# RWKV scan: the repeated values come from DRAM by DMA instead of through PE, and the four products of a token mix stand side by side in PE

## The chip, the cores and the metric

The program runs on one core of a Trainium2 chip. The metric is the device time of one execution in microseconds. PE is the matrix engine, DVE the vector engine, ACT the scalar engine, POOL the GpSimd engine; SP issues most DMAs. SBUF is the on-chip memory, PSUM the memory that PE writes to[...].

## What is computed

The reference applies four blocks in sequence to an activation `x` of 16 sequences x 100 steps x 512 channels, all float32: a grouped-query cross attention (layer 0), an RWKV block (layer 1), a cross attention with a feed-forward part (layer 2), and a second RWKV block (layer 3). The change touches the two RWKV blocks. Cut to what matters, such a block is

```python
xa = ln(x); sx = previous step of xa - xa
xxx = tanh((xa + sx * maa_x) @ maa_w1).reshape(b, l, 5, 32)     # five inner vectors of 32
xm = xa + sx * (maa_stack + einsum('blfd,fde->blfe', xxx, maa_w2))
xk, xw, xv, xr, xg = five slices of xm
w = exp(-exp(time_decay + tanh(xw @ td_w1) @ td_w2))
r, k, v, g = xr @ Wr.T, xk @ Wk.T, xv @ Wv.T, silu(xg @ Wg.T)
def step(s, (r_t, k_t, v_t, w_t)):                              # per head: 32 heads of 16
    a = k_t[:, None] * v_t[None, :]
    out = einsum('hi,hij->hj', r_t, u * a + s)
    return a + w_t[:, None] * s, out
x1 = x + groupnorm(out) * g @ Wo.T
return x1 + sigmoid(xr2 @ Wfr.T) * (square(relu(xk2 @ Wfk.T)) @ Wfv.T)
```

So the state of a head is a 16 x 16 matrix, and each of its 256 entries runs a linear recurrence over the 100 steps.

## The kernel before

The 16 sequences are cut into NG = 4 groups of G = 4 sequences, and the 512 channels into NC = 4 slices of 128. One tile of a group is [128, T] with T = 4 x 100 = 400 columns. `rwkv(n, ...)` builds one RWKV layer.

**Projections** (`projections(g, base)`). For a group it makes the normalised, transposed activation, the mixing input `xm`, the five inner vectors (`inner`, tanh; four of them in tile `z0` on partitions 0 to 127, the fifth in `tz`), the five mixes (`mixed(f, c)`: one matmul with 32 contraction rows for each of 5 vectors and 4 channel slices; then `scalar_tensor_tensor` on DVE into `tm` and an addition on POOL into `xj`), and the matmul chains of k, decay, v, r and g. k, v, r, w, g go to DRAM by `store` on ACT's queue, laid out [slice, 4, 32, T] so that a tile of 128 rows is contiguous.

**Units.** A chunk C is one group and one channel slice: 16 chunks of 8 units in a layer, so 128 units. In one unit u each partition scans two rows of 400 columns:

- `spread(u)` (PE): two matmuls of 32 rows with a 0/1 matrix `sel` repeat the values v over the partitions, into a PSUM tile `vb`, shifted by one step; an ACT copy writes the initial state into the first step of each sequence.
- `product(u)` (DVE): `vb` times the repeated k (`kr`), in place in PSUM, 128 x 792.
- `scan(u)`: two `tensor_tensor_scan` on DVE, reading the repeated decay `wr` and `vb`, writing SBUF tile `a`; then one POOL multiplication of `a` by the repeated r (`rr`), 128 x 800.
- `gather(p)` (PE): four matmuls for a pair of units, summing into the PSUM bank `acc`.

`repeat(C, rp)` fetches `kr`, `wr`, `rr` from DRAM: for each of the three, four DMAs of 32 partitions. `enter(C)` fetches the unrepeated tiles `vc`, `kc`, `rc`; `gates` fetches `gc`. `bonus` and `norm` add the u term and the group norm, with POOL multiplications `rk`, `og`, `gc`.

**Order.** The loop over u starts at -42 and writes every engine's program order by hand: DVE, ACT, POOL and PE instructions go through wrappers (line 77 for DVE, ACT and POOL, line 82 for matmuls, line 85 for transposes) that keep program order. In each unit the loop emits `spread(u + 1)`, `product(u)`, the deferred readers of PSUM banks, `scan(u)`, the loads of the next chunk, `gather`, and then as many filler pieces of PE work (projections of the next group, output projection, and in the last 34 units the channel-mixing half) as a budget `due` allows: 2.5, 2.95 or 3.9 us of PE work a unit. Group 0's projections stand before unit 0; the last group's channel mixing follows unit 127. PSUM holds two `vb` tiles of two banks, `acc`, and three banks `mm` for everything else, taken in turn by `Slots`.

Of the kernel before, what the change touches and what calls it, by code (L numbers as in the profile page):

```python
# [35 lines left out]
def xattn_sequence(ctx: ExitStack, tc: tile.TileContext, d: dict, out: bass.AP):  # L36
# [42 lines left out]
    vector, scalar, gpsimd = InOrder(nc.vector), InOrder(nc.scalar), InOrder(nc.gpsimd)  # L79
# [80 lines left out]
    class Slots:  # L160
# [22 lines left out]
        def read_later(self, bank, fn):  # L183
            once = self.readers[id(bank)] = self.defer(1, fn)
            return once
# [450 lines left out]
    def rwkv(n, ws, next_weights, last):  # L636
# [6 lines left out]
        with ExitStack() as es:  # L643
# [6 lines left out]
            vbs = [psum.tile([128, 2, 512], F32, name=f"vb{i}") for i in range(2)]  # L650
            acc = psum.tile([128, 512], F32, name="acc")
            slots = Slots([psum.tile([128, 512], F32, name=f"mm{i}") for i in range(3)])
# [3 lines left out]
            w2a = one.tile([128, E], F32, name="maa_w2a")  # L656
            nc.sync.dma_start(out=w2a, in_=d[f"L{n}_maa_w2"][0:128, :])

            w2b = one.tile([96, E], F32, name="td_maa_w2")
            nc.sync.dma_start(out=w2b[:64], in_=d[f"L{n}_td_w2"])  # L660
            nc.sync.dma_start(out=w2b[64:], in_=d[f"L{n}_maa_w2"][128:160, :])
# [26 lines left out]

            fold = one.tile([128, 32], F32, name="fold")
            nc.vector.tensor_reduce(fold, ident.rearrange("p (r s) -> p s r", s=32), AX.X, ALU.add)  # L690
            sel = one.tile([128, 16, 32], F32, name="sel")
            for j in range(16):
                nc.vector.tensor_copy(
                    sel[:, j, :].rearrange("p (h i) -> p h i", i=16),
                    fold.rearrange("p (h j) -> p h j", j=16)[:, :, j : j + 1].to_broadcast([128, 2, 16]),
                )
# [101 lines left out]

            def projections(g, base):
                nm = f"{n}_{g}"  # L800
                to = put[g] = {
                    t: dram.tile([NC, 4, 32, T], F32, tag=t, name=f"d{t}_{nm}")
                    for t in ("k", "v", "r", "w", "g")
                }

                def store(t, c, tile):
                    nc.scalar.dma_start(out=to[t][c].rearrange("r p t -> (r p) t"), in_=tile)
# [48 lines left out]
                def inner(lo, hi):  # L856
                    p0, z = (0, "z0") if lo == 0 else (64, "tz")
                    rs = slice(p0, p0 + hi - lo)
                    chain(
                        2.7, late, None, soon, lambda ps: ps[rs, :T], lambda c: w1[:, c, lo:hi],  # L860
                        lambda c: st["xm"][:, c, :],
                        lambda ps: scalar.activation(st[z][rs, :], ps[rs, :T], AF.Tanh),
                    )

                def mixed(f, c):

                    if c == 0:
                        xj[f] = two.tile([128, NC, T], F32, tag="xm", bufs=3, name=f"xj_{nm}_{f}")
                    ps = slots.bank()
                    cols = slice(c * 128, (c + 1) * 128)  # L870
                    rs = slice(32 * f, 32 * f + 32) if f < 4 else slice(64, 96)
                    w, z = (w2a, st["z0"]) if f < 4 else (w2b, st["tz"])
                    mm(out=ps[:, :T], lhsT=w[rs, cols], rhs=z[rs, :], start=True, stop=True)

                    def read():
# [6 lines left out]
                    mixes[f].append(slots.read_later(ps, read))  # L882
# [61 lines left out]
                mix = lambda f, c: piece(0.67, lambda: mixed(f, c), late)  # L944
                inner(0, 128)
                mix(0, 0)
                inner(128, 160)
                for c in range(1, NC):
                    mix(0, c)
                mix(1, 0)  # L950
                mix(1, 1)
                plain(0, "Wk", "k", 0)
                plain(0, "Wk", "k", 1)
                mix(1, 2)
                plain(0, "Wk", "k", 2)
                mix(1, 3)
                plain(0, "Wk", "k", 3)
                mix(2, 0)
                decay_in()
                for c in range(NC):  # L960
                    if c:
                        mix(2, c)
                    piece(0.67, lambda c=c: decay(c), late)
                for f, w, t in ((2, "Wv", "v"), (3, "Wr", "r")):
                    for c in range(NC):
                        mix(f + 1, c)
                        plain(f, w, t, c)
# [3 lines left out]
            def channels(g, slot):  # L971
# [41 lines left out]
                def keys(co):  # L1013
                    def read(ps):
                        if co == 0:
                            st["kk"] = two.tile([128, NC, T], F32, tag="kk", bufs=1, name=f"kk_{nm}")
# [19 lines left out]
                def values(i):  # L1036
                    b = g * G + i

                    def read(ps):
                        def add():  # L1040
# [3 lines left out]
                            if last:  # L1044
                                nc.sync.dma_start(out=out[b], in_=xb[b])
# [43 lines left out]
            def enter(C):  # L1089
# [4 lines left out]
                for k, bufs in (("v", 2), ("k", 1), ("r", 1)):  # L1094
                    t[k] = two.tile([128, T], F32, tag=f"{k}c", bufs=bufs, name=f"{k}c_{n}_{C}")
                    nc.sync.dma_start(out=t[k], in_=put[g][k][c].rearrange("r p t -> (r p) t"))
                repeat(C, 0)

            def repeat(C, rp):
                g, c = C // NC, C % NC  # L1100
                rep = chunks[C]["rep"][rp] = {}
                for t in ("k", "w", "r"):
                    rep[t] = two.tile([128, 2, T], F32, tag=f"{t}rep", bufs=3, name=f"{t}r_{n}_{C}_{rp}")
                    for jq in range(4):
                        nc.sync.dma_start(
                            out=rep[t][32 * jq : 32 * jq + 32],
                            in_=put[g][t][c, 2 * rp : 2 * rp + 2].rearrange("r p t -> p r t"),
                        )
# [23 lines left out]
            def spread(u):  # L1132

                C, jg, rp = where(u)
                p4 = vbs[u % 2][:, :, :T].rearrange("p r (b t) -> p r b t", t=L)
                for i in range(2):
                    rs = slice(64 * rp + 32 * i, 64 * rp + 32 * i + 32)
                    mm(
                        out=p4[:, i, :, 1:L], lhsT=sel[rs, 4 * jg : 4 * jg + 4, :].rearrange("p q m -> p (q m)"),
                        rhs=steps(chunks[C]["v"][rs, :])[:, :, 0 : L - 1], start=True, stop=True,  # L1140
                    )
                g = C // NC
                scalar.copy(
                    p4[:, :, :, 0], s0r[:, 2 * rp : 2 * rp + 2, C % NC, jg, g * G : (g + 1) * G]
                )

            def product(u):
                C, jg, rp = where(u)
                p4 = vbs[u % 2][:, :, :T].rearrange("p r (b t) -> p r b t", t=L)
# [6 lines left out]
            def scan(u):  # L1156
                C, jg, rp = where(u)
                rep = chunks[C]["rep"][rp]
                a = products[u] = two.tile([128, 2, T], F32, tag="a", bufs=4, name=f"a_{n}_{u}")
                for i in range(2):  # L1160
                    vector.tensor_tensor_scan(
                        a[:, i, :], rep["w"][:, i, :], vbs[u % 2][:, i, :T], 0.0, ALU.mult, ALU.add
                    )
# [39 lines left out]
            def gates(C):  # L1203
# [4 lines left out]
                nc.sync.dma_start(out=chunks[C]["g"], in_=put[g]["g"][c].rearrange("r p t -> (r p) t"))  # L1208
# [22 lines left out]
            while u < UNITS + 6 or pieces or slots.due:  # L1231
# [15 lines left out]
                if u == UNITS - 32 - 3:  # L1247
                    cm.update(load(n, "Wfk", "Wfr", "Wfv"))
                if u >= UNITS and not nws and not any(p[3] == ("wo", NG - 1) for p in pieces):
                    nws.update(next_weights())  # L1250
                unit = 0 <= u < UNITS
                if 0 <= u + 1 < UNITS:
                    spread(u + 1)
# [6 lines left out]
                if 0 <= C < NC * NG:  # L1260
                    if at == 4:
                        enter(C)
                    elif at == 6:
# [433 lines left out]
```

## Time and profile before

| | |
|---|---|
| median of 3 runs | 3563.27 us (3559.06 to 3570.37) |
| the profiled execution, its time | 3563.91 us |
| its span | 3561.8 us |
| PE busy | 3252.8 us (91% of the span) |
| DVE busy | 1768.5 us (50%) |
| POOL busy | 1374.2 us (39%) |
| ACT busy | 972.8 us (27%) |
| DMA | 213.26 MB, mean 60 GB/s |
| units of layer 1 | first product at 859.5 us, last scan ends at 1506.3 us |
| units of layer 3 | first product at 2819.4 us, last scan ends at 3465.5 us |

The busy time of an engine is the union of its instructions over the span[...]. The table's shares are means over stages with different limits; a stage is read from its own window. A group of the profile is named out<-in with the tiles of the program, "vb<-vc,sel" for instance is the matmul of `spread`. A float32 matmul appears as two instructions.

### The profile page before, as it was taken

The numbers are of one execution on the slowest core, as the hardware profiler recorded it, in microseconds if no ns is written. First come the engines' busy times: TensorE is split into PE (matmuls) and PEld (weight loads), VectorE is DVE, ScalarE is ACT, GpSimd is POOL, SyncE is SP. The second block draws the span as 40 slices with busy tenths as digits, with TensorE's granted clock in tenths as the row PEclk, the third lists the DMA queues.
The fourth block names the chain that finished last, engine by engine and source line by source line (L and its number), as shares of the span: only waits on it lengthen the run. The fifth ranks groups of instructions, "written<-read, shape, count | busy, mean of one in ns | idle before, by whom it ended". The sixth has DMA issues, their size and how long they took to land. (4 is left out here: it accounts for less than half of the span.)

```text
span 3561.8 us, 45408 instructions
## 1 busy us (share of the span) xinstructions
PE 3252.8 (91%) x17411; PEld 1434.5 (40%) x17411; DVE 1768.5 (50%) x3570; ACT 972.8 (27%) x1699; POOL 1374.2 (39%) x1036
## 2 busy tenths in 40 slices
PE   6999998868999988989999999699998899998898
PEld 3444443334333333334455455344443433333333
DVE  4777777723767755523333333400001386775551
ACT  1323222322333333322222322201111233333332
POOL 1444444543666655412212112200002366665541
PEclk8999999978999989989999999899998899998998
DMA  5010101022434342011000010200011243434300
GB/s 167 21 30 21 30 21 33 1 65 82 134 101 136 116 130 77 14 52 35 19 19 19 27 31 21 74 0 0 0 47 49 83 138 101 136 116 119 86 27 16
DMA packets 151074, 213.26 MB, mean 60 GB/s; under 512 B 22942, under 2 KB 131294, under 8 KB 150858
## 3 DMA queue, kind: packets, MB, share of 16 engines
q1 hardware_dynamic: 127818, 177.59, 17.3%
q10 hardware_dynamic: 23040, 32.78, 2.6%
q8 instruction: 137, 2.24, 0.3%
q14 instruction: 79, 0.65, 0.1%
HBM read 174.25 MB, written 36.04 MB: 59 GB/s over the span
## 5 line engine op out<-in xcount | busy, mean ns | idle before, releaser
L77 POOL TENSOR_TENSOR a<-a,rr 128x800 f32<-128x800 f32 x256 | 480.5, 1878 | 342.1 <-DVE a L77 265.4
L77 DVE TENSOR_TENSOR_SCAN a<-wr,vb 128x400 f32<-128x400 f32 x512 | 475.7, 970 | 19.3 <-PE acc L82 9.7
L77 DVE TENSOR_TENSOR vb<-vb,kr 128x792 f32<-128x792 f32 x256 | 250.5, 979 | 197.1 <-ACT vb L77 195.5
L77 DVE CUSTOM_DVE_ANT_0 junk<-l_sc,mask 100x361 f32<-100x361 f32 x512 | 273.0, 533 | 89.9 <-PE l_sc L82 73.4
L82 PE MATMUL vb<-vc,sel 32*128 32x396 f32 x1024 | 260.8, 566 | 2.4 <-ACT th L77 1.3
L77 DVE TENSOR_TENSOR pt<-l_sc,maskT 121x400 f32<-121x400 f32 x384 | 193.5, 566 | 91.9 <-PE l_sc L82 91.0
L77 ACT ACTIVATE pt<-pt 121x1600 f32<-121x1600 f32 x96 | 147.6, 1538 | 284.2 <-DVE pt L77 282.6
L1425 DVE CUSTOM_DVE_ANT_0 junk<-l2a_sc,mask 100x361 f32<-100x361 f32 x256 | 136.9, 535 | 173.0 <-PE l2a_sc L82 155.8
L63 PE MATMUL p<-l_proj,h 128*100 128x512 f32 x512 | 220.4, 593 | 0.0
L77 POOL TENSOR_TENSOR xj<-tm,ext 128x400 f32<-128x400 f32 x160 | 152.5, 960 | 170.3 <-DVE tm L77 165.2
L77 DVE SCALAR_TENSOR_TENSOR tm<-mm,vec,sx 128x400 f32<-128x400 f32 x160 | 99.8, 631 | 229.3 <-PE mm L82 184.3
L1617 DVE TENSOR_TENSOR x<-p,x 100x512 f32<-100x512 f32 x16 | 11.1, 691 | 379.3 <-PE p L63 340.2
L1461 POOL TENSOR_TENSOR pa<-pt,pt 121x1600 f32<-121x1600 f32 x16 | 57.2, 3573 | 366.7 <-ACT pt L1456 366.7
L63 PE MATMUL h<-yTb,l_fc 128*128 128x400 f32 x512 | 175.4, 505 | 7.9 <-ACT yTb L229 7.9
L82 PE MATMUL v<-l_v_w,ct 128*121 128x512 f32 x384 | 179.9, 614 | 0.0
L82 PE MATMUL k<-ct,l_k_w 128*128 128x361 f32 x512 | 172.8, 481 | 7.7 <-DVE mv_l2a L207 7.7
L77 POOL TENSOR_TENSOR pa<-pt,pt 121x1600 f32<-121x1600 f32 x32 | 114.7, 3583 | 167.0 <-ACT pt L77 167.0
L82 PE MATMUL l_sc<-kz,qz 32*100 32x361 f32 x1024 | 116.0, 523 | 42.6 <-DVE pt L77 21.6
L77 ACT COPY vb<-s0r 128x8 f32<-128x8 f32 x256 | 43.1, 168 | 408.7 <-PE vb L82 318.6
L82 PEld LDWEIGHTS vb<-vc,sel 32*128 32x128 f32 x1024 | 85.3, 190 | 145.5 <-issue 105.3
L63 PEld LDWEIGHTS p<-l_proj,h 128*100 128x100 f32 x512 | 85.7, 167 | 133.2 <-issue 132.6
L63 PEld LDWEIGHTS h<-yTb,l_fc 128*128 128x128 f32 x512 | 98.4, 193 | 82.9 <-ACT yTb L229 9.8
(254 smaller groups left out, 5317.3 us busy)
## 6 DMA issues: line engine op xcount, KB each, us to landing
kr<-dk SPq DMA_DIRECT2D x256, 100.0 KB
wr<-dw SPq DMA_DIRECT2D x256, 100.0 KB
rr<-dr SPq DMA_DIRECT2D x256, 100.0 KB
ct<-in_ctxT SPq DMA_DIRECT2D x32, 722.0 KB
dk<-k ACTq DMA_DIRECT2D x32, 200.0 KB
kc<-dk SPq DMA_DIRECT2D x32, 200.0 KB
dw<-wd ACTq DMA_DIRECT2D x32, 200.0 KB
dv<-v ACTq DMA_DIRECT2D x32, 200.0 KB
```

The lines of the kernel that those rows point to most:

```text
L63: nc.tensor.matmul(out=ps, lhsT=lhs(c), rhs=rhs(c), start=(c == 0), stop=(c == n - 1))
L77: return lambda *args, **kw: tc.keep_in_program_order(op(*args, **kw))
L82: pin(nc.tensor.matmul(**kw))
L1425: nc.vector.tensor_tensor_reduce(out=junk, in0=ss[r][:L, :S2], in1=t["mask"], scale=-1.0, scalar=FLT_MAX, op0=ALU.add, op1=ALU.min, accum_ ...
L1461: nc.gpsimd.tensor_tensor(t["pa"], t["pt"][0], pt, ALU.add)
L1617: nc.vector.tensor_tensor(x, ps[:L, :], x, ALU.add)
```

## The change

- `spread` goes. `fetch(u)` on SP's queue reads v from DRAM, every row 16 times, straight into the SBUF tile `a` of the unit, two units ahead; `a` has 6 buffers instead of 4. v lies in DRAM shifted by one element and in another row order, so that its store and its plain load are four DMAs of 32 partitions each. `first(u)` writes the initial state into `a` with ACT, one unit ahead. `product` and both scans now work in place in `a`.
- k, r, w, g lie in DRAM as [slice, 32, 4, T]. `repeat` fetches each repeated tile with one DMA, the fourfold repetition being the outermost dimension of its DRAM access, and the six of a chunk are spread over five units.
- A mix is one piece: `hidden(f)` copies the 32 rows of an inner vector onto the four groups of 32 partitions by four DMAs, and `mixed(f)` issues the four slices' matmuls on the four groups into four banks, one behind the other. The weights `w2a` are laid out to match. The readers of the banks are spread over two units.
- The PSUM of `vb` becomes four more banks for the turn: 7 instead of 3.
- DMAs inside the loop go through a wrapper that keeps SP's program order. Three weight matrices of the channel mixing are loaded in quarters over twelve units. `kk` shares the buffers of `xm`; `vc` has one buffer; the matrix `sel` is no longer built. The `due` budgets are as before.

```diff
-            vbs = [psum.tile([128, 2, 512], F32, name=f"vb{i}") for i in range(2)]
-            slots = Slots([psum.tile([128, 512], F32, name=f"mm{i}") for i in range(3)])
+            slots = Slots([psum.tile([128, 512], F32, name=f"mm{i}") for i in range(7)])
...
+            def rows_of(g, t, c):
+                if t == "v":
+                    n0 = 1 + c * 128 * T
+                    rows = put[g]["v"][n0 : n0 + 128 * T].rearrange("(j h r t) -> r h j t", h=2, r=4, t=T)
+                    return [(slice(32 * r, 32 * r + 32), rows[r]) for r in range(4)]
+                return [(slice(0, 128), put[g][t][c].rearrange("p r t -> r p t"))]
...
-                    t: dram.tile([NC, 4, 32, T], F32, tag=t, name=f"d{t}_{nm}")
-                    for t in ("k", "v", "r", "w", "g")
+                    t: dram.tile([NC, 32, 4, T], F32, tag=t, name=f"d{t}_{nm}")
+                    for t in ("k", "r", "w", "g")
...
-                    nc.scalar.dma_start(out=to[t][c].rearrange("r p t -> (r p) t"), in_=tile)
+                    for ps, rows in rows_of(g, t, c):
+                        nc.scalar.dma_start(out=rows, in_=tile[ps])
...
+                def hidden(f):
+                    z = st["z0"][32 * f : 32 * f + 32, :] if f < 4 else st["tz"][64:96, :]
+                    t = st["zr", f] = two.tile([128, T], F32, tag="zr", bufs=2, name=f"zr_{nm}_{f}")
+                    for c in range(NC):
+                        sync.dma_start(out=t[32 * c : 32 * c + 32, :], in_=z)
+
+                def mixed(f):
...
+                    for c, ps in enumerate(banks):
+                        rs = slice(32 * c, 32 * c + 32)
+                        mm(out=ps[:, :T], lhsT=w2a[rs, f, :], rhs=st["zr", f][rs, :], start=True, stop=True)
...
-            def repeat(C, rp):
-                rep = chunks[C]["rep"][rp] = {}
-                for t in ("k", "w", "r"):
+            def repeat(C, rp, names):
+                rep = chunks[C]["rep"].setdefault(rp, {})
+                for t in names:
                     rep[t] = two.tile([128, 2, T], F32, tag=f"{t}rep", bufs=3, name=f"{t}r_{n}_{C}_{rp}")
-                    for jq in range(4):
-                        nc.sync.dma_start(
-                            out=rep[t][32 * jq : 32 * jq + 32],
-                            in_=put[g][t][c, 2 * rp : 2 * rp + 2].rearrange("r p t -> p r t"),
-                        )
+                    k = put[g][t][c, :, 2 * rp : 2 * rp + 2, :]
+                    sync.dma_start(
+                        out=rep[t], in_=bass.AP(k.tensor, k.offset, [[0, 4], [4 * T, 32], [1, 2 * T]])
+                    )
...
-            def spread(u):
-                p4 = vbs[u % 2][:, :, :T].rearrange("p r (b t) -> p r b t", t=L)
-                for i in range(2):
-                    rs = slice(64 * rp + 32 * i, 64 * rp + 32 * i + 32)
-                    mm(
-                        out=p4[:, i, :, 1:L], lhsT=sel[rs, 4 * jg : 4 * jg + 4, :].rearrange("p q m -> p (q m)"),
-                        rhs=steps(chunks[C]["v"][rs, :])[:, :, 0 : L - 1], start=True, stop=True,
-                    )
+            def fetch(u):
+                a = products[u] = two.tile([128, 2, T], F32, tag="a", bufs=6, name=f"a_{n}_{u}")
+                v = put[g]["v"]
+                n0 = v.offset + ((c * 16 + 4 * jg) * 8 + 2 * rp) * T
+                sync.dma_start(out=a, in_=bass.AP(v.tensor, n0, [[4 * T, 8], [0, 16], [1, 2 * T]]))
+
+            def first(u):
                 scalar.copy(
-                    p4[:, :, :, 0], s0r[:, 2 * rp : 2 * rp + 2, C % NC, jg, g * G : (g + 1) * G]
+                    products[u].rearrange("p r (b t) -> p r b t", t=L)[:, :, :, 0],
+                    s0r[:, 2 * rp : 2 * rp + 2, C % NC, jg, g * G : (g + 1) * G],
                 )
...
-                    vector.tensor_tensor_scan(
-                        a[:, i, :], rep["w"][:, i, :], vbs[u % 2][:, i, :T], 0.0, ALU.mult, ALU.add
-                    )
+                    vector.tensor_tensor_scan(a[:, i, :], rep["w"][:, i, :], a[:, i, :], 0.0, ALU.mult, ALU.add)
                 gpsimd.tensor_tensor(a, a, rep["r"], ALU.mult)
...
+                if 0 <= u + 2 < UNITS:
+                    fetch(u + 2)
                 if 0 <= u + 1 < UNITS:
-                    spread(u + 1)
+                    first(u + 1)
                 if unit:
                     product(u)
...
                     if at == 4:
                         enter(C)
+                    elif at == 5:
+                        repeat(C, 0, "w")
                     elif at == 6:
-                        repeat(C, 1)
+                        repeat(C, 0, "r")
                         bonus(C, 0)
                     elif at == 7:
+                        repeat(C, 1, "kw")
                         bonus(C, 1)
                 C = u // 8
+                if 0 <= C < NC * NG and at == 0:
+                    repeat(C, 1, "r")
```

## The prediction

> **What bounds the kernel now.** I read the page's busy times first (PE 91%), then the stretches of the units, because only the RWKV layers change. Layer 1's units 0 to 92, then 93 to 127, all instructions; columns are busy us of PE, PEld, DVE, ACT, POOL, then granted clock, DMA share, GB/s:
>
> ```profile
> 859.40:1285.90 426.50, 412.32 (x1560) 156.37 (x1561) 312.97 (x385) 136.01 (x288) 283.44 (x228) 0.94 0.41 120
> 1285.90:1506.40 220.50, 196.00 (x665) 72.51 (x664) 127.03 (x158) 77.57 (x150) 117.34 (x99) 0.90 0.21 57
> ```
>
> The first stretch is PE's: 412 of 426 us, 4.59 us a unit (426.5 / 93). The second takes 6.30 us a unit (220.5 / 35). Layer 3 repeats both within 1 us. The same stretch for `vb` on PE, for the product (with `kr`), and for four of the five mixes (`z`, PE first):
>
> ```profile
> 859.40:1285.90 426.50, 94.55 (x372) 0.94 0.41 120
> 859.40:1285.90 426.50, 91.00 (x93) 0.94 0.41 120
> 859.40:1285.90 426.50, 44.68 (x96) 15.00 (x96) 1.51 (x3) 0.94 0.41 120
> ```
>
> So the spread costs PE 1.02 us a unit. The mixes cost 44.7 us, plus a quarter for the fifth vector: 56 us, 0.60 a unit. DVE (313) and POOL (283) have room, and run side by side: together 6.4 us of work in 4.59 us. That rests on `vb` being in PSUM. Where a DVE instruction has both inputs in SBUF, the timeline shows something else:
>
> ```profile
> 1350.32 1.88 POOL L77 TENSOR_TENSOR a<-a,rr 128x800 f32<-128x800 f32 x1 [0.96 <-DVE a L77]
> 1351.67 1.08 DVE L77 SCALAR_TENSOR_TENSOR x<-th_1b,x 100x512 f32<-100x512 f32 x1
> 1352.15 1.48 POOL L77 TENSOR_TENSOR gc<-gc,og 128x400 f32<-128x400 f32 x1
> 1352.67 1.85 DVE L77 TENSOR_TENSOR_SCAN a<-wr,vb 128x400 f32<-128x400 f32 x2
> ```
>
> `x<-th_1b,x` normally takes 0.69 us. Here it ends 0.55 us after POOL's `a` (1352.20), and `gc`, normally 1.06, ends 0.88 us after it. They take turns, with about 0.15 us of overlap at a handover. The scans, whose `vb` is in PSUM, make nobody wait.
>
> Last, the DMAs. One store of 100 rows, then one weight load of 512 rows, each alone; I show packets and the load's GB/s by slice:
>
> ```profile
> DMA packets 110, 0.20 MB, mean 34 GB/s; under 512 B 10, under 2 KB 10, under 8 KB 110
> DMA packets 528, 1.05 MB, mean 150 GB/s; under 512 B 16, under 2 KB 16, under 8 KB 528
> GB/s 0 0 0 0 0 0 0 140 105 187 187 293 176 257 293 363 386 410 421 421 421 386 398 410 328 211 152 47 0 0 0 0 0 0 0 0 0 0 0 0
> ```
>
> The small packets are one completion for each DMA engine used: 10 engines for 100 rows, 16 for 512 (128 partitions). At the peak 16 engines move 421 GB/s, 26.3 GB/s each.
>
> [...]
>
> **The change, part by part.**
>
> *PE.* It loses 1.02 us a unit of spread and three quarters of the mixes (0.45): 4.43 busy - 1.47 = 2.96 us a unit. Before unit 0, 20 mix calls of 0.94 us become 5, less waits for the new copies: I take -8 us a layer (-14 to +4). Building `sel` (16 copies of 0.17 us) was off the path: nothing.
>
> *DVE and POOL.* Product and scans now read two SBUF inputs. Their own durations I keep: product 0.98 us, two scans 1.85 us. [...] But they exclude POOL's 283.4 / 93 = 3.05 us: 2.83 + 3.05, less three handovers of 0.15, is 5.4 us a unit; in the last 35 units POOL has 117.3 / 35 = 3.35, so 5.7. Bounds: no exclusion for scans at one end (then DVE's own 3.4), no overlap and some gaps at the other (6.2).
>
> *DMA: the largest term.* For each new access I take the leading dimension. A repeated tile, [4 x 32 x 800]: 4 engines. A fetch, [8 x 16 x 800]: 8. k, r, w, g in and out, [4 x 32 x 400]: 4. v in and out, [2 x 16 x 400]: 2. [...] per chunk each of them carries:
>
> - six repeated tiles of 409.6 KB / 4: 614 KB
> - eight fetches of 409.6 KB / 8: 410 KB
> - `kc`, `rc`, `gc`, 204.8 KB / 4 each: 154 KB
> - v's plain load, 204.8 KB / 2: 102 KB
> - while projections run, four stores / 4 and v's / 2: 205 + 102 KB
>
> The sum is 1587 KB, at 26.3 GB/s 60 us for 8 units, 7.5 us a unit. Without stores it is 1280 KB, 49 us, 6.1 a unit. Before, every one of these used 16 engines (32 or 128 leading rows), hence a DMA share of 0.41 only. The new mean, some 0.95 MB a unit, looks harmless as well; it is the uneven split that counts. If instead all DMAs used 16 engines, 0.95 MB at 421 GB/s is 2.3 us a unit and hidden.
>
> *Waits and queues.* Product now waits for `first` on ACT, and that for the fetch. Behind it on ACT stand the tanh, the copies of k, v, r and the store issues; PE's banks and SP's `hidden` wait for those. SP is one ordered queue: a fetch waits for the gather of the unit six before, and the second `kr`, `wr` for the scan just before their issue, so the queue cannot always be kept full. SP's issue count stays about the same (28 a chunk before, 26 with 5 of `hidden`, at 0.4 us). The `hidden` copies have 32 leading rows, 16 engines, 0.1 us each: small. The quartered weight loads carry the same bytes. `kk` in the `xm` ring and the single `vc` wait only for readers long done: nothing, and one unit's wait if that cover goes.
>
> *Sum.* I add 10% for gaps in the DMA rings (0 to 25%), a choice, since PE's queue before kept 97% and a chain of DMA, compute and buffer release should do worse: 8.25 us a unit, then 6.7. Per layer: 93 x (8.25 - 4.59) = +340; 35 x (6.7 - 6.3) = +14; before unit 0: -8. About +348, twice +696. The tail after unit 127 is unchanged. The profiled execution took 3563.9 us (span 3561.8; median of the runs 3563.3), so 3563.9 + 696 = **4260 us**. With no gaps 93 x 2.91 - 35 x 0.2 - 14 = +250 a layer, about 4060; with 25% (9.4 and 7.6) about 4550.
>
> **The rivals.** *Turns only:* the DMAs do spread, or the engines chosen rotate, and DVE and POOL set the pace. 93 x (5.4 - 4.59) - 35 x 0.6 - 8 = +46 a layer up to 93 x (6.2 - 4.59) - 8 = +142: 3656 to 3848, about **3720**. For it: the turns are in the trace[...].
>
> *Faster:* DMAs spread and scans don't exclude POOL. Then DVE's 3.4 us plus some turns of the product alone, about 3.9 us a unit, replaces PE's 4.59, and the last 35 units lose the spread (about -1.0): -64 - 35 - 8 = -107 a layer, about **3350**. It decides where both new prices are below 4.59 us a unit. Against it: the scan has two SBUF inputs like `x<-th_1b,x`.
>
> *The mixes don't stand side by side:* PE keeps 0.45 us a unit, still below 3.5, and nothing moves in the first two cases.
>
> **How the numbers follow.** Few engines 0.70, turns only 0.20, faster 0.10. The point is the first case's 4260; its own range is 4060 to 4500. The 8-in-10 range reaches down over the turns case: 3650 to 4500. About 0.3% is what a measurement of this kernel can tell from no change. Faster by more 0.09, within 0.02, slower by more 0.89.
>
> **What would show it.** Few engines: on ACT's queue each of the 128 stores of k, r, w, g counts 128 + 4 packets and each of the 128 parts of v 32 + 2, in all 128 x 132 + 128 x 34 = 21248 (160 x 144 = 23040 before; 24576 if all used 16 engines). Pace near 8 us a unit, `first` or the product waiting for the fetch, DMA share under 0.5. Turns: product and POOL's `a` above 0.98 and 1.88 us in the mean. A pace below 4.6 us refutes both; 5.4 to 6.2 with the small counts would say that the split is right and its price wrong.

## The result, and the profile after

The changed kernel takes **4384.8 us** (median of 4 runs, 4378.6 to 4399.1), the kernel before beside it 3564.2 us. The ratio is 1.231 (95% interval 1.227 to 1.234): 821 us slower. The profiled execution has a span of 4380.6 us, against 3561.8.

The time is lost in the units of the two RWKV layers. These are the stretches of layer 1's units 0 to 92 and 93 to 127 in the changed kernel, with the columns of the prediction's first fence (busy us of PE, PEld, DVE, ACT, POOL, then granted clock, DMA share, GB/s):

```profile
860.90:1660.80 799.90, 377.61 (x1222) 145.31 (x1222) 417.26 (x388) 140.33 (x298) 354.39 (x235) 0.70 0.34 116
1660.80:1912.20 251.40, 179.38 (x522) 68.08 (x522) 160.55 (x156) 77.08 (x151) 148.50 (x100) 0.78 0.35 116
```

No engine is near full: PE 378 of 800 us, DVE 417, POOL 354, and the DMA share is 0.34. (DVE and POOL together are busy for 772 us, so turns between these two could fill the stretch as well; e5 below decides that.) A unit takes 799.9 / 93 = 8.60 us instead of 4.59, and in the second stretch 251.4 / 35 = 7.18 instead of 6.30. From the first product to the last scan, layer 1 takes 1051.3 us (1912.2 - 860.9) instead of 646.8, layer 3 1067.3 instead of 646.1: 404.5 + 421.2 = 826 us, which is the whole loss.

Three groups of the page (busy us, mean ns of one, idle before them and what ended most of it):

```profile
L77 DVE TENSOR_TENSOR_SCAN a<-wr,a 128x400 f32<-128x400 f32 x512 | 684.9, 1378 | 237.3 <-ACT a L77 125.9
L77 POOL TENSOR_TENSOR a<-a,rr 128x800 f32<-128x800 f32 x256 | 534.7, 2093 | 681.4 <-DMA rr<-dr 386.7
L77 DVE TENSOR_TENSOR a<-a,kr 128x792 f32<-128x792 f32 x256 | 321.9, 1257 | 625.3 <-DMA a<-dv 425.4
```

The same three in the kernel before:

```profile
L77 DVE TENSOR_TENSOR_SCAN a<-wr,vb 128x400 f32<-128x400 f32 x512 | 475.7, 970 | 19.3 <-PE acc L82 9.7
L77 POOL TENSOR_TENSOR a<-a,rr 128x800 f32<-128x800 f32 x256 | 480.5, 1878 | 342.1 <-DVE a L77 265.4
L77 DVE TENSOR_TENSOR vb<-vb,kr 128x792 f32<-128x792 f32 x256 | 250.5, 979 | 197.1 <-ACT vb L77 195.5
```

DVE and POOL do take turns now: the three groups are busy for 209, 54 and 71 us longer. But the idle time before them grew by more, 218, 339 and 428 us. For POOL's `a` and the product most of it ends with a DMA, for the scans half of it with ACT's copy. A selection of the waits (us in total, times, longest); the lines with SPq are from the waits of SP's queue:

```profile
ACT a L77 <- DMA a<-dv: 1015.6, 144, 23.1
PE mm L82 <- POOL rk L77: 513.6, 30, 30.1
DVE a L77 <- DMA a<-dv: 425.4, 89, 17.4
POOL a L77 <- DMA rr<-dr: 386.7, 32, 20.7
...
SPq L77 <- PE acc L82: 328.2, 45, 19.1
...
SPq L77 <- DMA a<-dv: 118.7, 56, 12.0
...
SPq L77 <- DMA wr<-dw: 90.9, 22, 7.6
SPq L77 <- DMA rr<-dr: 88.0, 18, 6.9
```

The fetches `a<-dv` are late, the repeated `rr` too. `PE mm <- POOL rk` is the bonus' matmul: it was 17.8 us in all before. SP's `PE acc` is a fetch that waits for a gather to free its buffer of `a`. The last three lines, 298 us together, are SP waiting for other DMAs to land, although its next DMA does not need their data. The semaphore events in the trace tell why: the 1274 DMAs that SP and ACT issue share eight semaphores, and in all 1266 pairs that follow each other on one semaphore the first had landed before the second's issue ended. So at most eight DMAs were in flight. In units 0 to 92 of layer 1 all eight were for 27% of the time, in the kernel before for 1%. One slow DMA held up issues that had nothing to do with it.

The timeline shows how these hang together:

```profile
988.47 11.69 ACTq L813 DMA_DIRECT2D dv<-v  x4
...
997.62 1.87 POOL L77 TENSOR_TENSOR a<-a,rr 128x800 f32<-128x800 f32 x1
...
999.02 1.30 DVE L77 TENSOR_TENSOR a<-a,kr 128x792 f32<-128x792 f32 x1 [10.39 <-DMA a<-dv]
1000.20 0.20 ACT L77 COPY a<-s0r 128x8 f32<-128x8 f32 x1 [14.58 <-DMA dv<-v]
1000.30 0.62 ACT L77 ACTIVATE kc<-kc,vec 128x400 f32<-128x400 f32 x1
...
1001.00 1.24 POOL L77 TENSOR_TENSOR rk<-rc,kc 128x400 f32<-128x400 f32 x1 [1.52 <-ACT kc L77]
...
1002.30 1.70 PE L82 MATMUL mm<-rk,ones 128*128 128x400 f32 x2 [19.84 <-POOL rk L77]
...
1003.93 1.56 PE L82 MATMUL acc<-a,gat 128*32 128x400 f32 x8
...
1010.08 1.28 SPq L77 DMA_DIRECT2D a<-dv  x1
```

DVE waited 10.4 us for a fetch, ACT 14.6 us before its `first`. In that time ACT issued four stores of v, 0.6 us each, and waited for DMAs to land between them: the third started at 998.94, just after a fetch had landed at 998.92. Behind `first` on ACT stands `kc`, behind that POOL's `rk`, then PE's bonus matmul, which held PE's ordered queue for 19.8 us. The gather follows, and only later does SP issue the next fetch. A late DMA thus delays the release of the buffer for a later one. POOL's and DVE's first lines also show a turn: the product, 0.98 us alone, ends 0.83 us after POOL's `a` (999.49).

Last, the row of the page for ACT's DMA queue (packets, MB, share):

```profile
q10 hardware_dynamic: 21248, 32.77, 2.2%
```

21248 packets is the count that the prediction worked out for 4 and 2 engines. That the leading dimension sets this number, and that all such DMAs meet on the same few engines, was its author's assumption: no DMA of SP or ACT in the kernel before has fewer than 11 semaphore events. The semaphore events of the trace after bear out the first. A DMA with a leading dimension of 2, 4 or 8 has one event more than that: 3 for each part of v, 5 for each repeated tile and for each store and plain load of k, r, w, g, 9 for each fetch. A copy of `hidden`, with 32, has 16, as all DMAs of k, v, r, w, g have in the kernel before; a load or store of 100 rows has 11.

The packets' times say how busy the few engines were. (During the prediction's lone store and weight load, ten and sixteen packets at a time were the commonest counts above zero, as many as their small packets.) In units 0 to 92 of layer 1 at least one packet was under way for 98% of the time, exactly four for 44% and more than eight for 9%. While no DMA in flight led with more than 4 (81 us of the stretch), four packets or fewer were under way for 85% of the time and never more than seven, although the leading dimensions of those in flight added up to 18.6 in the mean. While the largest was 8 (470 us), eight or fewer were for 93%, never more than twelve, with a mean sum of 29.9. So these DMAs did not add up, as if they shared their engines. Which engine carried a packet the trace does not say.

### The profile page after: what moved, and what is told of

The parts are those of the page before. It is cut to its first block, busy times and chain, and to the rows that moved or that the text cites. A ratio compares the mean times of both kernels' runs of the same rounds, so it can differ in the third digit from the quotient of the medians.

```text
span 4380.6 us, 43662 instructions
## 1 busy us (share of the span) xinstructions
PE 3094.9 (71%) x16387; PEld 1381.0 (32%) x16387; DVE 2041.9 (47%) x3536; ACT 967.7 (22%) x1699; POOL 1567.8 (36%) x1036
## 3 DMA queue, kind: packets, MB, share of 16 engines
q1 hardware_dynamic: 134138, 290.61, 19.8%
q10 hardware_dynamic: 21248, 32.77, 2.2%
## 5 line engine op out<-in xcount | busy, mean ns | idle before, releaser
L77 DVE TENSOR_TENSOR_SCAN a<-wr,a 128x400 f32<-128x400 f32 x512 | 684.9, 1378 | 237.3 <-ACT a L77 125.9
L77 POOL TENSOR_TENSOR a<-a,rr 128x800 f32<-128x800 f32 x256 | 534.7, 2093 | 681.4 <-DMA rr<-dr 386.7
L77 DVE TENSOR_TENSOR a<-a,kr 128x792 f32<-128x792 f32 x256 | 321.9, 1257 | 625.3 <-DMA a<-dv 425.4
L82 PE MATMUL mm<-rk,ones 128*128 128x400 f32 x64 | 54.2, 950 | 513.6 <-POOL rk L77 513.6
L77 ACT COPY a<-s0r 128x8 f32<-128x8 f32 x256 | 51.6, 202 | 1319.7 <-DMA a<-dv 1015.6
L77 POOL TENSOR_TENSOR xj<-tm,ext 128x400 f32<-128x400 f32 x160 | 202.4, 1288 | 110.7 <-DVE tm L77 110.7
L82 PE MATMUL acc<-a,gat 128*32 128x400 f32 x1024 | 166.9, 619 | 56.0 <-POOL a L77 52.4
L82 PE MATMUL acc<-rk,center 128*32 128x400 f32 x256 | 44.7, 787 | 222.2 <-ACT sq L77 222.2
L82 PEld LDWEIGHTS mm<-rk,ones 128*128 128x128 f32 x64 | 16.1, 313 | 533.7 <-POOL rk L77 533.7
L82 PE MATMUL mm<-xj,l_Wk 128*128 128x400 f32 x256 | 108.1, 565 | 59.5 <-POOL xj L77 59.2
```

The lines of the kernel that those rows point to most:

```text
L77: return lambda *args, **kw: tc.keep_in_program_order(op(*args, **kw))
L82: pin(nc.tensor.matmul(**kw))
```

## The experiments

The pace below is in us a unit, units 0 to 92, then 93 to 126, of layer 1, worked out from the starts of the products in each trace. "DMA on 16 engines" means that the leading dimension of its access in DRAM is 16 or 32; the packet counts of e1 and e2 below show 16 completions for each such DMA.

| run | us | ratio (95%) | pace |
|---|---|---|---|
| before | 3564 | 1 | 4.59, 6.28 |
| after | 4384.8 | 1.231 (1.227–1.234) | 8.60, 7.26 |
| e1_repeats16 | 4182.1 | 1.173 (1.165–1.181) | 7.97, 6.57 |
| e8_loads_stores16 | 4333.0 | 1.216 (1.212–1.219) | 8.23, 7.44 |
| e2_all16 | 3967.1 | 1.113 (1.108–1.117) | 6.73, 6.38 |
| e5_no_r_multiply | 4355.6 | 1.222 (1.218–1.226) | 8.49, 7.39 |
| e6_all16_no_r_multiply | 3843.3 | 1.078 (1.075–1.081) | 6.18, 6.02 |
| e7_all16_gather_first | 3952.2 | 1.109 (1.106–1.112) | 6.69, 6.27 |
| e9_all16_first_on_dve | 3959.4 | 1.109 (1.107–1.112) | 6.70, 6.47 |
| e10_all16_first_dve_late_bonus | 3971.1 | 1.113 (1.111–1.116) | 6.73, 6.53 |
| e11_after_first_on_dve | 4359.9 | 1.223 (1.220–1.226) | 8.49, 7.22 |
| e12_all16_old_shapes | 3893.4 | 1.092 (1.090–1.094) | 6.44, 6.45 |
| e3_scan_from_sbuf | 3688.4 | 1.034 (1.030–1.039) | 5.13, 6.59 |
| e4_mix_pairs_on_before | 3508.7 | 0.984 (0.979–0.989) | 4.50, 6.07 |

### Are the few engines the cause? e1, e2

e1 is the changed kernel with each repeated tile loaded by four DMAs of 32 partitions:

```diff
-                    sync.dma_start(
-                        out=rep[t], in_=bass.AP(k.tensor, k.offset, [[0, 4], [4 * T, 32], [1, 2 * T]])
-                    )
+                    for jq in range(4):
+                        sync.dma_start(out=rep[t][32 * jq : 32 * jq + 32], in_=k)
```

> Only the repeated tiles (kr, wr, rr) go back to four DMAs of 32 partitions each, from the new DRAM layout, so that their leading dimension is 32 and 16 engines take them; everything else is the changed kernel. Few engines: [...] the turns of DVE and POOL (5.4 to 6.2 us) are next. Pace 5.6 to 6.6 us a unit, time about 3850 us (3700 to 4000). If the bytes or the wait for the fetch are what costs, whatever the spread: unchanged at about 4385 us, since the same bytes move.

e2 adds the same for every other short leading dimension. v is stored twice, so that the fetch leads with 16:

```diff
-                    return [(slice(32 * r, 32 * r + 32), rows[r]) for r in range(4)]
-                return [(slice(0, 128), put[g][t][c].rearrange("p r t -> r p t"))]
+                    return [
+                        (slice(32 * r + 16 * h, 32 * r + 16 * h + 16), rows[i, r, h])
+                        for i in range(copies) for r in range(4) for h in range(2)
+                    ]
+                return [(slice(32 * r, 32 * r + 32), put[g][t][c, :, r, :]) for r in range(4)]
...
-                sync.dma_start(out=a, in_=bass.AP(v.tensor, n0, [[4 * T, 8], [0, 16], [1, 2 * T]]))
+                sync.dma_start(out=a, in_=bass.AP(v.tensor, n0, [[4 * T, 16], [0, 8], [1, 2 * T]]))
```

> As the run with the repeated tiles on 16 engines, and all other DMAs too: k, r, w, g stored and loaded by four DMAs of 32 partitions; v stored twice in DRAM, so that a fetch's leading dimension is 16 (16 rows, each read 8 times), its parts stored and loaded by 16 partitions. Few engines: 7.8 MB a chunk over 16 engines is 486 KB each, 18.5 us or 2.3 us a unit, so DMA no longer sets the pace and the turns of DVE and POOL do: 5.4 to 6.2 us a unit, 3656 to 3848 us, about 3750; products and scans stay longer than 0.98 and 0.97 us in the mean. Without turns: below 4.6 us a unit, about 3350 us. If bytes or the wait for the fetch cost: 4385 us or more, since a second copy of v is stored.

Measured: 4182 and 3967 us. So 203 us come back with the repeated tiles alone, 418 with all DMAs spread: half of the loss. Both misses are on the same side: e1 was expected at 3850 and e2 in the turns' range up to 3848. ACT's queue in e2 tells that the spreading happened, 40960 packets:

```profile
q10 hardware_dynamic: 40960, 39.39, 3.6%
```

512 parts of 32 rows (k, r, w, g) with 16 completions each and 512 parts of 16 rows (v, twice) with 16 each give just that: 512 x 48 + 512 x 32.

The same row for SP's queue, after, e1, e2:

```profile
q1 hardware_dynamic: 134138, 290.61, 19.8%
```

```profile
q1 hardware_dynamic: 145658, 290.66, 24.9%
```

```profile
q1 hardware_dynamic: 157306, 290.70, 28.6%
```

The 11520 packets that e1 adds are 192 repeated tiles with 64 completions instead of 4. The 11648 that e2 adds are 256 fetches (16 instead of 8), 96 loads of k, r and g (64 instead of 4) and 32 of v (128 instead of 8). So the repeated tiles and the fetches, too, ran on the 4 and 8 engines for which the prediction had no trace.

SP's row for the fetches in the tile view of `a` (min, median and max ns of one issue) shows the pressure going away. After, e1, e2:

```profile
L77 SPq DMA_DIRECT2D a<-dv x256: 574/804/7382, 833.4 to 4272.2; - x128
```

```profile
L77 SPq DMA_DIRECT2D a<-dv x256: 574/592/705, 839.9 to 4060.6; - x128
```

```profile
L77 SPq DMA_DIRECT2D a<-dv x256: 513/519/829, 847.8 to 3854.8; - x128
```

In the changed kernel one issue took up to 7.4 us. Where ACT waited for a fetch, the time from the end of its issue to ACT's copy was 13.6 us in the median after, 6.8 in e1, 4.2 in e2.

### Which of the few-engine DMAs? e8

The changed kernel with only the stores and plain loads spread (the second `return` of e2's edit, with v in parts of 16 rows stored once, and `gc` to match).

> The changed kernel with only the stores and the plain loads of k, r, w, g and v spread over 16 engines (four DMAs of 32 partitions, v eight of 16); repeated tiles stay on 4 engines and fetches on 8. [...] as in the run with the repeated tiles on 16 (1127 KB). If the load of the busiest engines is what counts: about the same time as there, 4180 us, within 80. If it is the place in SP's queue (v's and the plain loads in front of the fetch of the chunk's last unit, a hole of some 16 us in the product's pace there): that hole shrinks below 9 us and the time goes to 4050 us or less.

4333 us: 52 of the 821. Neither number was met. By the prediction's kind of sum, e1 and e8 leave nearly the same bytes on the busiest engines while projections run: for e1, 410 (fetches) + 154 (repeated tiles / 16) + 154 + 102 (loads) + 307 (stores) = 1127 KB a chunk; for e8, 614 + 410 + 51 + 64 = 1139 KB. At 26.3 GB/s that is 5.4 us a unit for either. They took 7.97 and 8.23 us in the first stretch. (In the second, without the stores, e8 has more on these engines, 1075 KB against 820, and is slower, 7.44 against 6.57.) So the sum is wrong for both. Either the load of the busiest engines is not what counts, or 26.3 GB/s, read from one weight load, is too high a rate. SP's row for e8 beside those above speaks for the rate:

```profile
q1 hardware_dynamic: 143738, 290.65, 22.2%
```

The bytes are the same in all four, the packets' time is not: 19.8% of 16 engines over the span is 13.9 ms, and 16.6 in e1, 15.4 in e8, 18.1 in e2. A busy engine thus moved 20.9, 17.5, 18.9 and 16.0 GB/s in the mean. An estimate from these rates puts the busiest engines at 9.5 us a unit in the changed kernel, 8.1 in e1 and 7.5 in e8; measured were 8.60, 7.97 and 8.23. At least one packet was under way for 92% of the first stretch in e1 and in e8. So the load of the busiest engines fits within some 10% again, at a lower rate, and is not ruled out. Why packets take longer when more engines are at work is not shown.

The place in SP's queue may count beside the load: e8 left the median from a fetch's issue to ACT's copy at 13.5 us, e1 halved it.

### Do DVE's and POOL's turns set the pace? e3, e5, e6

e3 is the kernel before with the product writing to SBUF, so that only the scans have two SBUF inputs (their v still comes through PE and PSUM):

```diff
-                    p4[:, :, :, 1:L], p4[:, :, :, 1:L],
+                    products[u].rearrange("p r (b t) -> p r b t", t=L)[:, :, :, 1:L], p4[:, :, :, 1:L],
...
-                        a[:, i, :], rep["w"][:, i, :], vbs[u % 2][:, i, :T], 0.0, ALU.mult, ALU.add
+                        a[:, i, :], rep["w"][:, i, :], a[:, i, :], 0.0, ALU.mult, ALU.add
```

> The kernel before, with PE's spread kept: only the product writes its result into the SBUF tile a (5 buffers) instead of in place into PSUM, so that the two scans have two SBUF inputs; kk shares the buffers of xm to make room. Product still has one input in PSUM. Turns: the scans and POOL exclude each other; 1.85 + 3.05 less two handovers of 0.15 is 4.6 us a unit, just at PE's 4.59, so the mean scan grows to 1.1 us or more, POOL's a above 1.95, and the time to 3580 to 3700 us. No turns for scans: scan 0.97 us, POOL's a 1.88 us and the time 3564 us within 0.5%.

3688 us, as expected: +123. The groups of its page:

```profile
L77 DVE TENSOR_TENSOR_SCAN a<-wr,a 128x400 f32<-128x400 f32 x512 | 687.5, 1382 | 8.7 <-ACT sq L77 0.5
L77 POOL TENSOR_TENSOR a<-a,rr 128x800 f32<-128x800 f32 x256 | 483.4, 1889 | 378.7 <-DVE a L77 307.6
L77 DVE TENSOR_TENSOR a<-vb,kr 128x792 f32<-128x792 f32 x256 | 245.9, 961 | 181.7 <-PE vb L82 131.8
```

A scan grew from 970 to 1382 ns when its second input moved from PSUM to SBUF. The SBUF input alone doesn't slow it: the 150 scans that overlap no POOL instruction took 968 ns in the mean (993 at most), the other 362 took 1554; before, both kinds took 968 to 971. POOL's `a` stayed at 1889 ns, the product, with one input in PSUM, at 961. So a scan with two SBUF inputs takes turns with POOL, which for scans was the prediction's assumption.

e5 and e6 leave out the multiplication by r on POOL (one column of each row is set to zero instead), in the changed kernel and in e2:

```diff
-                gpsimd.tensor_tensor(a, a, rep["r"], ALU.mult)
+                gpsimd.memset(a[:, :, 0:1], 0.0)
```

> The changed kernel with POOL's multiplication of a by the repeated r left out (256 instructions of 1.88 us; POOL writes one column of a instead, which reads nothing; rr is still loaded). It asks whether, in the changed kernel, the DMA engines or the turns set the pace. Few engines: [...] the time stays above 4150 us. Turns: DVE's 2.83 us and POOL's other 1.2 us are 4.0 us a unit, and up to 256 x 1.9 = 480 us go: 3900 to 3950 us.

> The run with all DMAs on 16 engines, again without POOL's multiplication by r. There the turns should set the pace of 6.6 us a unit, or else SP's ordered queue does. Turns: 4.0 us a unit of DVE and POOL together, PE 3.0, so 4.2 to 5.0 us a unit and 3450 to 3650 us. Ordered queue (fetches wait for gathers that stand on PE behind the product of the bonus, and behind loads that wait): pace stays above 6 us a unit, 3850 us or more.

Without the multiplication the changed kernel gains 29 us, e2 gains 124. The turns are there in both, but in the changed kernel DVE and POOL take them in time that they would spend waiting for DMAs. That decides between the prediction's case and its first rival: with few engines, DMA sets the pace. It also says that e2's remaining 402 us are not mainly turns with POOL's `a`: 280 of them remain in e6.

### What holds e2 at 6.7 us a unit? e7, e9, e10, e11, e12

With all DMAs on 16 engines and a turns price of 5.4, something still costs 1.3 us a unit. I tried four single suspects.

e7 issues PE's gather right behind the scan, ahead of the next chunk's loads and the bonus, so that buffers come free earlier:

```diff
+                if u % 2 and 0 <= (u - 3) // 2 < UNITS // 2:
+                    gather((u - 3) // 2)
```

> The run with all DMAs on 16 engines, with the gather issued right behind the scan of its unit, ahead of the next chunk's loads and of the bonus product, which waits on PE for POOL's rk (288 us in that run) with the gather, and so the next fetch, behind it. Ordered queue: the loop fetch - ACT - rk - bonus product - gather - next fetch opens, the pace goes from 6.6 to 5.6 - 6.2 us a unit, 3750 to 3880 us. Turns alone: 3967 us within 1%.

e9 moves the copy of the step-0 column from ACT to DVE, away from ACT's store issues; e11 does that to the changed kernel. The copy stands just ahead of its unit's product:

```diff
-                if 0 <= u + 1 < UNITS:
-                    first(u + 1)
                 if unit:
+                    first(u)
                     product(u)
...
-                scalar.copy(
+                vector.tensor_copy(
```

> e2_all16 (3967.1 us) with the copy of the step-0 column moved from ACT to DVE, behind the product of its own unit, so that no scan stands behind ACT's store issues (16 parts of v: 9.3 us each time on ACT). In e2 DVE waited 238.0 us for ACT's copy in the scans; the copy adds 256 x some 0.1 us to DVE. If ACT's order is what keeps e2 above the turns' price: 3967 - 238 + 26 = 3755, at most 3850. If SP's one ordered queue does it (its repeated tiles, loads and fetches, each with waits): 3930 or more, with the waits gone over to the fetch.

> The changed kernel (4384.8 us) with that copy moved from ACT to DVE alone; the DMAs stay on few engines. There ACT waited 1015.6 us for the fetch before the copy. If the few engines set the pace, DVE waits for the same fetches instead: 4300 to 4400. If ACT's order behind its stores and copies is the cost, 4250 or less.

e10 is e9 with the bonus two units later:

```diff
-                        bonus(C, 0)
                     elif at == 7:
                         repeat(C, 1, "kw")
-                        bonus(C, 1)
...
                     repeat(C, 1, "r")
+                    bonus(C, 0)
+                if 0 <= C < NC * NG and at == 1:
+                    bonus(C, 1)
```

> The kernel of e9 with the bonus' first two steps (POOL's rk, PE's product of it) issued at units 0 and 1 of their own chunk instead of units 6 and 7 of the chunk before, which is when their loads have just been asked for. In e2 PE waited 287.7 us for rk, and SP's fetches waited 285.7 us for PE's gathers (buffers of a). If that chain (late load, rk, PE, gather, buffer, fetch) costs time: 60 to 150 us under e9. If the fetches' own place in SP's queue decides, within 20 us of e9.

e12 is e9 with the DRAM layout of the kernel before for k, r, w, g, and v stored there a third time for its plain load, so that these stores and the plain loads are one DMA each on 16 engines:

```diff
-                return [(slice(32 * r, 32 * r + 32), put[g][t][c, :, r, :]) for r in range(4)]
+                return [(slice(0, 128), put[g][t][c].rearrange("r p t -> (r p) t"))]
...
-                    for ps, rows in rows_of(g, t, c, 2):
+                    for ps, rows in rows_of(g, t, c, 2) + (rows_of(g, "vp", c) if t == "v" else []):
```

> The kernel of e9 with k, r, w and g laid out in DRAM as in the kernel before, and v stored there once more in that layout for its plain load: still 16 engines for every DMA, but one DMA of 128 rows where e9 has four or eight. SP then issues some 5.0 DMAs a unit instead of 7.04 (3.14 us of issue a unit in e9, expected 2.2), ACT 21 a chunk instead of 32. If the number of issues in SP's one queue holds the fetches back, 0.9 us a unit over 2 x 93 to 2 x 128 units: 3959 - 170 to - 230, so 3730 to 3790, a pace near the turns' 5.4. If it is the waits between them in a fixed order (for the gathers' buffers, the stores to DRAM, the scans' tiles), 3900 or more.

Measured: e7 -15 us against e2; e9 -8, or 0.2%, too little to build on; e10 +12 against e9; e11 -25 against the changed kernel. In e9, DVE's waits for ACT's copy and for the fetch fell from 238.0 + 97.9 = 336 us to 167.3, and the time did not follow: in layer 1, DVE's waits for PE at `rk` and `tm` rose from 52 to 100 us. In e11 they were 513.7 us, against 125.9 + 425.4 = 551 in the changed kernel. All three theories of a single wait fell; e11 came out as the few-engine theory had it. It also tells against the chain through `kc`: with `first` gone from ACT, PE still waited 479.5 us for `rk`, against 513.6.

e12 gained 66 us on e9, where fewer issues were to bring 170 to 230, and lies just under the 3900 of the other answer. SP's DMAs in its first stretch took 2.40 us of issue a unit instead of 3.14 (1.35 in the kernel before, 4.14 in the changed one; summed from the traces). So the number of issues costs something, and most of the rest does not come from it. Its trace has a stall of 20.5 us between two products, with this in it:

```profile
965.29 8.06 ACTq L818 DMA_DIRECT2D dv<-v  x16
...
973.87 0.63 ACT L77 ACTIVATE kc<-kc,vec 128x400 f32<-128x400 f32 x1 [8.61 <-DMA dv<-v]
...
974.57 1.03 POOL L77 TENSOR_TENSOR rk<-rc,kc 128x400 f32<-128x400 f32 x1 [6.14 <-ACT kc L77]
...
975.65 1.70 PE L82 MATMUL mm<-rk,ones 128*128 128x400 f32 x2 [17.45 <-POOL rk L77]
...
977.39 0.57 DVE L77 TENSOR_TENSOR rk<-mm,vc 128x400 f32<-128x400 f32 x1 [17.16 <-PE mm L82]
...
978.93 0.52 SPq L77 DMA_DIRECT2D a<-dv  x1
```

The 16 stores of v, a number which exists only because e2's family writes v in parts of 16 rows twice, hold ACT for 8 us. `kc` stands behind them, then POOL's `rk`, PE's bonus, DVE's product with it and the gather, and SP issues its next fetch after that. In e12 PE waited 265 us for `rk` in 30 waits; in 8 of them, 76 us in all, `kc` was late, so this stall is not typical. The chain is read from the trace. A version with fewer stores of v was not run, nor one that lets more than eight DMAs be in flight (all eight were for 14% of the first stretch in e2, 13% in e12). So how much of e12's 328 us over the kernel before either costs **stays open**, and with it how fast the fetch could be with every other cost gone.

### The mixes alone: e4

The kernel before with the change's inner vectors on four partition groups, the mixes in pairs (its three banks have no room for four), and the order of the pieces around them fitted to that:

```diff
-                def mixed(f, c):
+                def mixed(f, h):
...
-                    mm(out=ps[:, :T], lhsT=w[rs, cols], rhs=z[rs, :], start=True, stop=True)
+                    banks = {c: slots.bank() for c in (2 * h, 2 * h + 1)}
+                    for c, ps in banks.items():
+                        rs = slice(32 * c, 32 * c + 32)
+                        mm(out=ps[:, :T], lhsT=w2a[rs, f, :], rhs=st["zr", f][rs, :], start=True, stop=True)
```

> The kernel before with the second part of the change alone, as far as its three PSUM banks allow: inner values copied onto four groups of 32 partitions by DMA (32 leading rows, 16 engines), and a mix's four products issued as two pairs side by side on different row groups; kk shares the buffers of xm. v still goes through PE. Side by side: PE loses half of the mixes' 0.60 us a unit, 93 x 0.3 = 28 us a layer, and some 7 us before unit 0: about 3495 us (3470 to 3530). Not side by side, or the copies' wait comes back on PE: 3564 us or up to 3600.

3508.7 us, 0.984 of the kernel before (0.979 to 0.989). Its two stretches:

```profile
849.50:1268.00 418.50, 404.15 (x1570) 153.57 (x1570) 313.88 (x387) 137.29 (x288) 281.79 (x227) 0.94 0.44 129
1268.00:1480.00 212.00, 191.89 (x663) 70.67 (x664) 123.98 (x156) 76.99 (x151) 119.93 (x101) 0.93 0.22 60
```

The first product starts 10 us earlier (849.5 instead of 859.5), and PE still fills 404 of 418.5 us: where PE is the bound, less PE work is worth its time. The five mixes take PE 30.9 us in the first stretch here and 19.3 in the changed kernel, instead of about 56: they do stand side by side. That they would was the prediction's assumption. In the changed kernel the four calls of a mix take 0.954 us together (median of 40 mixes), as long as one call in the kernel before (0.935). This version is 1.6% faster than the kernel before.

## Why the prediction was right, and where it was not

- **The bound before** and PE's relief. PE was the bound, and PE lost the spread's 372 instructions and most of the mixes' time (x1560 to x1222 in the first stretch). So the rival in which the mixes don't stand side by side fell. The 2.96 us a unit of PE did not come: 377.6 / 93 = 4.06. A matmul instruction now takes 377.6 / 1222 = 309 ns instead of 264, at a granted clock of 0.70 instead of 0.94. PE was idle for more than half of the stretch by then; what the slower clock cost in the chain through the bonus and the gather is not shown.
- **Few engines**, the likeliest case: confirmed. The packet counts are exact; a pace of 8.60 against 8.25 predicted, then 7.18 against 6.7; DMA share 0.34, under 0.5; `first` and the product waiting for the fetch. The gaps were sized at 10%; the paces make them 15% (8.60 / 7.5) and 18% (7.18 / 6.1). Per layer 404.5 and 421.2 us against 348 (its terms add up to 346).
- **The sum behind it** is only half right, and that 7.5 plus a chosen 10% came so near 8.60 is in part luck. For e1 and e8 the same sum gives 5.4, and they stayed at 7.97 and 8.23. The weak step is the rate of 26.3 GB/s an engine: the pages show 16.0 to 20.9 in the mean. What may count as well is the ring: a fetch waits for a buffer, the buffer for units that are late because of earlier fetches, and every issue for the landing of an earlier DMA. The prediction named SP's ordered queue and put it inside the 10%; the limit of eight DMAs in flight it did not have. SP's issue count stayed the same, as it said (3.3 a unit), but an issue took 1.2 us in the mean instead of 0.4.
- **Turns**: confirmed as a fact, by product, scans and `a` above their durations of before and by e3. The durations that the prediction kept for two SBUF inputs, 0.98 us for the product and 1.85 for two scans, stand near the changed kernel's medians of 984 ns and 2 x 992. Their price was somewhat low: for e3, with the product still outside, it gave 4.6 us a unit, and 5.13 were measured. POOL's `a` with its turns is worth 29 us in the changed kernel and 124 in e2.
- **If all DMAs used 16 engines, hidden**: not so. e2 has that, at 152 GB/s in its first stretch with a DMA share of 0.60, still waits for fetches, and is at 6.73, above the 6.2 at the rival's upper end. The 421 GB/s of the sum were the peak of one weight load.
- **-8 us before unit 0** did not come (860.9 instead of 859.5). e4 has -10, so the mixes give it, and so has e1 (850.0), though not e2 (860.1); what the first product waits for in the changed kernel I did not take apart.
- **Waits**: `first` was named as what the product waits for. The two touch different columns, and the product waits for the fetch itself (`DVE a <- DMA a<-dv`); the scans wait for `first`. Not named was `kc` behind `first` on ACT: in 26 of PE's 30 waits for `rk` it was late, for 436 of the 514 us. But e11 shows that freeing ACT of `first` brings little.
- **Faster**, the rival on the other side, needed scans that don't exclude POOL. e3 refutes that.

## What to carry to other kernels

Look at the leading dimension of every access before trusting a bandwidth sum: here much the same bytes from 4 or 8 engines instead of 16 cost 418 us (the changed kernel against e2), at a mean DMA share of 0.34 against 0.60. Price them with the rate of such a transfer, not with the peak of another one. When a value moves from an engine to a DMA in one ordered queue, follow the ring of issue, transfer, use and buffer release once around, through every engine's queue that it passes; spreading the bytes mends the transfer, not the ring. And try the parts of a change singly: the mixes side by side gained 1.6% and were buried under a loss of 23%.

## What the runs showed of the hardware

- The issue of a DMA on SP is not a fixed price: 574 ns at the least, 7382 ns at the most for the same fetch while the transfers ran on few engines, and 705 ns at the most in e1, with the repeated tiles on 16.
- More DMA engines at work moved less each: the same 290.6 MB of SP's queue went at 20.9 GB/s a busy engine in the changed kernel, 17.5 in e1 and 16.0 in e2.
- Where PE waited more, its granted clock was lower. The clock record has two values, full and half speed: 451 us of the span at half before, 1442 us after. After, PE was busy for 39% of the time at half speed and for 86% of the rest, before for 73% and 94%. The same bonus matmul `acc<-rk,center` has a median of 522 ns before and 874 ns after (874 / 522 = 1.67), where the first stretch has a mean clock of 0.94 and 0.70.
- Turns between a scan with two SBUF inputs and POOL cost now one, now the other: in e3 the scan's mean rose by 412 ns and that of POOL's `a` by 11; in e2, where the product has two SBUF inputs as well, by 499 and 325.
